# Third mixture of experts: where its zeros, edge rows, edge products and returned rows stand

## The chip, the cores and the metric

One core of a Trainium2 chip. The time is device microseconds of one launch; a kernel is compared by the median over runs. The profile is one execution taken by the hardware profiler; its times are microseconds from the start of the span unless marked ns. Engines: PE (TensorE, matmul), DVE (VectorE), ACT (ScalarE), POOL (GpSimd, which also issues indirect DMAs), SP (SyncE, which issues DMAs).

## The reference

The reference is a four-layer graph network over N = 2708 nodes with D = 256 features; every layer is a graph step over the dense adjacency and a feed-forward step, both added to x. The change lies in layer 2 (the third):

```python
x = x + _L2_gnn_ref(_layernorm(x), adj, W, a)        # one-head graph attention
x = x + _L2_ffn_ref(_layernorm(x)[None], ...)[0]      # mixture of 4 experts, this case

h = x @ W_gat                                          # (M, 4 heads, 4 experts)
e = leaky_relu(a_src[src] + a_dst[dst])                # over listed edges and self loops
alpha = segment softmax of e over dst
agg = segment_sum(h[src] * alpha, dst) + b_gat
scores = layernorm(agg).reshape(M, 4, 4).mean(1)
topk_s, topk_i = top_k(scores, 2);  w = softmax(topk_s)
for ei in range(4):
    g = where(topk_i == ei, w, 0).sum(-1)
    hh = gelu(x @ W1[ei] + b1[ei])                     # 256 -> 512
    out += g[:, None] * (hh @ W2[ei] + b2[ei])         # 512 -> 256
```

Layer 3 then starts with a four-head attention, whose values are prepared inside this mixture.

## The kernel before

The nodes lie in 22 tiles of 128 rows (the last has 20), and work goes by CHUNKS: five chunks of 512 nodes and one of 148. x stays in SBUF the whole time (k.x). The program is written once and then scheduled: a scheduler fixes, before anything runs, the order of the instructions on each engine, from the order in the text, the data dependencies and its own estimates. On the chip each engine goes through its list in that order and stops at an instruction whose inputs aren't there. So where an instruction stands in an engine's list can differ from where it stands in the text.

The parts that the change and the prediction touch, in order of time:

- **Before the one-head pass.** `load_x` (L71) reads x from the table `acc` in DRAM, that the mixture of layer 1 scatters into; each of its seven loads waits for the one two before it. `GatFront.all` norms x (L1641 to L1655), transposes it (`ft_ps`, L1610) and multiplies with the attention's weights (`v_ps`, L3447); the weights' last columns are made by DVE from `w` and the rows `ar` (L3432, L3438). `Deal.__init__` fills a zero tile on POOL (L4035) and has POOL write it to twelve places in DRAM: row 0 of four tables `fd` (L4040) and eight tables `z` of 512 rows (L4042).
- **The one-head pass** (`fast_gat`): for each chunk DVE makes the weights PT from the adjacency tile `aj` (L3551), PE multiplies (`acc_ps`, L3650), DVE normalizes and adds to x (L3686). Eight `aj` tiles and ten PT tiles are in turn.
- **Edge part of the mixture** (`scores_listed`). All edges that need it are in 16 columns of 128 rows (OW = 16). For each, POOL gathers a row of R from DRAM into `Rd` and one of T into `G` (L3855), 32 gathers in all, in two groups of Q = 8 columns. Then, per group, DVE forms `wq` (L3926), `msg` (L3867) and for each column an X of 128x440 (L3931), and PE adds them up in `e_ps` (L3939), 16 products. `S` (L3947), the norms, the two highest scores per node, and `Deal.rank` (L4108 to L4190) follow; they give the gates and the slots. `last_used` makes a flag that decides the branch at L4356, by which the fourth expert is skipped when no node picked it.
- **Experts.** `up` makes `h_ps` (L4266) and applies gelu on ACT (L4273); `down` makes `y_ps` (L4283), one tile of 128x256 per block of 128 nodes, in two buffers. Expert 0 runs on all six chunks while the edge part is going on; its results, and those of experts 1 and 2 on chunk 0, are parked: `park` copies y_ps by ACT (L4300) and adds the bias on POOL (L4301). The gathers wait in three places for a parked row: `scores.send` hands in a parked column, from which DVE makes a zero that is added to the row numbers (L3850, L3851).
- **Units.** For chunks 1 to 4 experts 1 and 2 run only on the rows dealt to them: eight units (c, i) of 384 or 256 rows. A unit gathers its rows (`xe`, L4196), transposes them (L4370), runs `up` and `down`, and for each block of y DVE adds the bias (`ys`, L4415) and POOL scatters it to `z` (L4210). `back(c)` loads both z of a chunk (`zt`, L4383, on SP), and `plus` adds its rows to x by DVE (L4344). In between `side` works off the steps of layer 3's values (L3483, L3447, L3453), a few at a time, one chunk after another, as soon as a chunk's x is complete.

Of the kernel before, what the change touches and what calls it, by code (L numbers as in the profile page):

```python
# [29 lines left out]
def blocks(c0, cs):  # L30

    return [((c0 + o) // 128, o, min(128, cs - o)) for o in range(0, cs, 128)]
# [3700 lines left out]
def scores_listed(k, fT, w, edges, agg, pool):  # L3733
# [3 lines left out]

    nc, tc = k.nc, k.tc
    H, E = 4, 4
    W = E + 2
# [3 lines left out]
    with ExitStack() as pc, tc.tile_pool(name="sp", bufs=1) as pp, tc.tile_pool(  # L3747
# [90 lines left out]
        for c0 in range(0, OW, Q):  # L3838
            for src, idx, out in (
                (Rt, edges.odst, Rd),  # L3840
                (Tt, edges.osrc, G.rearrange("p c h w -> p c (h w)")),
            ):


                at = idx[:, c0 : c0 + Q]
                done = yield
                if done is not None:
                    at = tmp.tile([128, Q], I32, name="at_idx")
                    no = tmp.tile([128, 1], I32, name="no")
                    nc.vector.tensor_tensor(no, done, done, ALU.is_lt)  # L3850
                    nc.vector.tensor_tensor(  # L3851
                        at, idx[:, c0 : c0 + Q], no.to_broadcast([128, Q]), ALU.add
                    )
                for c in range(Q):
                    nc.gpsimd.indirect_dma_start(  # L3855
                        out=out[:, c0 + c, :],
                        out_offset=None,
                        in_=src,
                        in_offset=bass.IndirectOffsetOnAxis(
                            ap=at[:, c : c + 1], axis=0  # L3860
                        ),
                        bounds_check=NT * 128 - 1,
                        oob_is_err=False,
                    )
# [48 lines left out]
        )  # L3913
        acc = ps.tile([128, NT, H * (E + 1)], F32, name="e_ps")
        for c0 in range(0, OW, Q):
            cc = slice(c0, c0 + Q)
            dlo = tmp.tile([128, Q, 128], F32, name="dlo")
            nc.vector.tensor_tensor(
                dlo,
                io[:, None, :].to_broadcast([128, Q, 128]),  # L3920
                edges.olo[:, cc, None].to_broadcast([128, Q, 128]),
                ALU.is_equal,
            )
            wq = tmp.tile([128, Q, H], F32, name="wq")
            msg = tmp.tile([128, Q, H, E + 1], F32, name="msg")
            nc.vector.tensor_tensor(wq, Rd[:, cc, :], G[:, cc, :, E + 1], ALU.max)  # L3926
            times(msg, wq, G[:, cc, :, : E + 1], Q)
            for c in range(Q):
                X = tmp.tile([128, NT, H * (E + 1)], F32, name="X")
                shp = [128, NT, H * (E + 1)]  # L3930
                nc.vector.tensor_tensor(  # L3931
                    X,
                    dhi[:, c0 + c, :, None].to_broadcast(shp),
                    msg[:, c, :, :]
                    .rearrange("p h w -> p (h w)")[:, None, :]
                    .to_broadcast(shp),
                    ALU.mult,
                )
                nc.tensor.matmul(  # L3939
                    acc.rearrange("p t w -> p (t w)"),  # L3940
                    lhsT=dlo[:, c, :],
                    rhs=X.rearrange("p t w -> p (t w)"),
                    start=(c0 + c == 0),
                    stop=(c0 + c == OW - 1),
                )
# [74 lines left out]
class Deal:  # L4020
# [8 lines left out]
    S = 5  # L4029

    def __init__(self, k, dram, pool):
        nc = k.nc
        self.k = k
        zero = pool.tile([128, 4, D], F32, name="zero")
        nc.gpsimd.memset(zero, 0.0)  # L4035
        self.fd, self.z = [], []
        for c in range(len(self.C)):
            self.fd.append(dram.tile([513, D], F32, name=f"fd{c}"))
            self.z.append([dram.tile([512, D], F32, name=f"z{c}{i}") for i in range(2)])
            nc.gpsimd.dma_start(self.fd[c][0:1, :], zero[0:1, 0, :])  # L4040
            for z in self.z[c]:
                nc.gpsimd.dma_start(z.rearrange("(t p) d -> p t d", p=128), zero)  # L4042
# [177 lines left out]
def fast_l2_ffn(k, w, edges, deal, then):  # L4220
# [7 lines left out]
    with ExitStack() as ctx:  # L4228
# [14 lines left out]
        ps1 = ctx.enter_context(tc.tile_pool(name="ps_m1", bufs=3, space=PSUM))  # L4243
        ps2 = ctx.enter_context(tc.tile_pool(name="ps_m2", bufs=2, space=PSUM))
        first = yp.tile([128, NT, D], F32, name="y0")
        whole = {e: yp.tile([128, 4, D], F32, name=f"y{e}") for e in (1, 2)}
        b1 = bp.tile([128, E, M], F32, name="b1")
        b2 = bp.tile([128, E, D], F32, name="b2")
        for e in range(E):
# [29 lines left out]
        def down(e, hT, bl, use):  # L4279
            for t, o, n in bl:  # L4280
                y = ps2.tile([128, D], F32, name="y_ps")
                for m in range(M):
                    nc.tensor.matmul(  # L4283
                        y[:n],
                        lhsT=hT[:, m, o : o + n],
                        rhs=wts[e][1][:, m, :],
                        start=(m == 0),
                        stop=(m == M - 1),
                    )
                use(t, n, y)  # L4290
                next(side[0], None)

        def expert(e, c0, cs, use):
            hT = up(e, lambda kk: fT[:, kk, c0 : c0 + cs], cs)
            down(e, hT, blocks(c0, cs), use)

        def park(e, dst):
            def use(t, n, y):
                yt = dst[:n, t, :]
                nc.scalar.copy(yt, y[:n])  # L4300
                nc.gpsimd.tensor_tensor(yt, yt, b2[:n, e, :], ALU.add)  # L4301

            return use

# [8 lines left out]
        with tc.tile_pool(name="el", bufs=1) as pl, tc.tile_pool(  # L4313
            name="eh2", bufs=2
        ) as hot, tc.tile_pool(name="ps_el", bufs=1, space=PSUM) as ps:
            deal.prepare(keep, pl, hot)
            bank = ps.tile([128, 512], F32, name="deal_ps")
            agg = pl.tile([128, NT, 4, 4], F32, name="agg")
            scores = scores_listed(k, fT, w, edges, agg, pl)
            next(scores)  # L4320
            next(scores)

            pace = iter((3, 4, 7))
            at = next(pace)
            for c0, cs in CHUNKS:
                expert(0, c0, cs, park(0, first))
                while at is not None and at < c0 // 128 + 4:
                    scores.send(first[:, at, :1])
                    at = next(pace, None)
            for _ in scores:  # L4330
                pass
            scores_norm(k, w, agg, sc, pl)
            top2_dense(k, sc, E, gates, pl)
            wts.update({e: load(e) for e in (2, 3)})
            for c in deal.rank(gates, bank):
                for i in range((2, 1, 0, 0)[c]):
                    xes[c, i] = gathered(c, i)
            last_used(k, gates[:, :, E - 1], flag, pl, deal.ids[:, 3, :1])
            for e in (1, 2):
                expert(e, *CHUNKS[0], park(e, whole[e]))  # L4340

        def plus(src, t, n, e):
            xt = k.x[:n, t, :]
# [47 lines left out]
        def drain():  # L4391
            for _ in side[0]:
                pass

        own(*CHUNKS[0])
        for e in (1, 2):
            for t in range(4):
                plus(whole[e][:, t, :], t, 128, e)
        side[0] = steps(*CHUNKS[0])
        units = [(c, i) for c in range(4) for i in range(2)]  # L4400
        xT = turn(*units[0])
        zs = {}
        for u, (c, i) in enumerate(units):
# [15 lines left out]
            xT = xT_next  # L4419
            if i == 1:  # L4420
                zs[c] = back(c)
            elif c > 0:
                drain()
                for j in range(2):
                    for t in range(4):
                        plus(zs[c - 1][j][:, t, :], deal.C[c - 1][0] // 128 + t, 128, 1 + j)
                side[0] = steps(*deal.C[c - 1])
        own(*CHUNKS[-1])
        expert(1, *CHUNKS[-1], add(1))
        drain()  # L4430
        for j in range(2):
            for t in range(4):
                plus(zs[3][j][:, t, :], deal.C[3][0] // 128 + t, 128, 1 + j)
        side[0] = steps(*deal.C[3])
        expert(2, *CHUNKS[-1], add(2))
        drain()
        for _ in steps(*CHUNKS[-1]):
            pass
# [417 lines left out]
def model(tc, I, out):  # L4856
# [4 lines left out]
    with tc.tile_pool(name="flags", bufs=1) as fp:  # L4861
# [4 lines left out]
        with ExitStack() as ctx:  # L4866
            k = Fast(ctx, tc, I["x"], bad, adjT)
            with tc.tile_pool(name="lists", bufs=1) as lp:
# [36 lines left out]
                with ExitStack() as c2:  # L4905
                    keep = c2.enter_context(tc.tile_pool(name="g2", bufs=1))
                    with tc.tile_pool(name="g2t", bufs=1) as tmp:
                        front = GatFront(k, I["L2_gnn_W"], I["L2_gnn_a"], 1, keep, tmp)
                        front.all(tmp)
                        front.ready(2)  # L4910
                    deal = Deal(k, dealt, keep)
                    fast_gat(k, adjT, front, True)
                c3 = ctx.enter_context(ExitStack())
                right = dict(side="right")
                keep = c3.enter_context(tc.tile_pool(name="g3", bufs=1, **right))
# [96 lines left out]
```

## Time and profile before

| | us |
|---|---|
| median of three runs | 2414.18 (2412.02 to 2417.53) |
| the profiled execution | 2414.3 |
| its span | 2412.5 |
| PE busy in it | 2235.9 |
| DVE busy in it | 1529.4 |
| ACT, POOL busy in it | 713.8, 444.2 |
| PE busy from 1485.0 to 1757.4 (the mixture) | 241.4 of 272.4 |
| PE busy from 1617.6 to 1757.4 (from the branch on) | 119.8 of 139.8 |
| PE busy from 1250.0 to 1440.0 (the one-head pass) | 189.95 of 190.0 |

A window's row gives its length, then for each engine the busy time and, in brackets, the number of instructions, then the granted PE clock, the DMA engines' busy share and the rate in GB/s. A wait's row gives the engine and line that waited, the engine and line that it waited for, and total, times and longest in us. In a timeline a row is a group of like instructions: start, length, engine, line, operation, tile written, tiles read, shape, count, and in brackets the idle time before it and what ended that. An engine that stands idle costs something only if PE, in the end, waits for it.

### The profile page before, as it was taken

The page shows a single profiled execution, that of the slowest core. Times are in us where ns is not written, and L with a number is a line of the kernel's source. Part 1 is how long each engine was busy: PE and PEld are TensorE (multiplying, and loading weights), DVE is VectorE, ACT ScalarE, POOL GpSimd, SP SyncE. Part 2 cuts the span into 40 slices and gives each one's busy share as a digit, 9 for nine tenths or more (in the row PEclk, how much of TensorE's full clock was granted, in tenths as well). Part 3 has the DMA queues.
Part 4 walks back from the last instruction along what each step waited for, and adds up shares of the span by engine and source line. Part 5 has one row for each costly group of instructions (what it writes and reads, how often), then busy time and mean ns, then how long its engine had stood idle before and what let it go on. Part 6 is the DMA issues. An engine that isn't in the chain of part 4 may idle for free. (4 is left out here: it accounts for less than half of the span.)

```text
span 2412.5 us, 32100 instructions
## 1 busy us (share of the span) xinstructions
PE 2235.9 (93%) x11600; PEld 1493.6 (62%) x11600; DVE 1529.4 (63%) x3453; ACT 713.8 (30%) x1499; POOL 444.2 (18%) x482
## 2 busy tenths in 40 slices
PE   7999999988899899999689998988899999959996
PEld 4777765677778676777568886647632333326664
DVE  7588878645676557456555554183489998854544
ACT  6433343213655222212150003333451112211221
POOL 1000013004100243565300001623100000012221
PEclk9999999869999999999889996999999999979998
DMA  5244332200756244332345535012233333324430
GB/s 150 66 114 118 110 79 78 74 1 12 236 172 191 62 115 97 82 75 49 106 147 146 144 84 102 13 40 75 66 90 104 109 112 110 92 69 146 134 116 15
DMA packets 168111, 235.23 MB, mean 98 GB/s; under 512 B 32125, under 2 KB 101475, under 8 KB 167940
## 3 DMA queue, kind: packets, MB, share of 16 engines
q1 hardware_dynamic: 130320, 184.03, 26.3%
q0 software_dynamic: 18688, 32.97, 6.1%
q10 hardware_dynamic: 18932, 16.05, 2.1%
q8 instruction: 95, 1.56, 0.3%
q14 instruction: 76, 0.62, 0.1%
HBM read 200.31 MB, written 33.74 MB: 97 GB/s over the span
## 5 line engine op out<-in xcount | busy, mean ns | idle before, releaser
L3551 DVE SCALAR_TENSOR_TENSOR PT<-Rr,Q,aj 128x512 f32<-128x512 f32 (+3 forms) x630 | 395.2, 680 | 102.6 <-PE acc_ps L3650 78.5
L3725 PE MATMUL acc_ps<-PT,V 128*64 128x512 f32 (+4 forms) x2016 | 333.3, 551 | 0.1
L3725 PEld LDWEIGHTS acc_ps<-PT,V 128*64 128x64 f32 (+1 forms) x2016 | 94.0, 122 | 210.2 <-issue 158.3
L1845 PE MATMUL acc_ps<-fa,PT 128*128 128x257 f32 x882 | 215.4, 383 | 1.2 <-DVE out L1865 1.2
L1845 PEld LDWEIGHTS acc_ps<-fa,PT 128*128 128x128 f32 x882 | 163.9, 190 | 66.5 <-issue 33.8
L3650 PE MATMUL acc_ps<-V,PT 128*128 128x257 f32 x882 | 194.3, 381 | 0.8 <-issue 0.8
L3650 PEld LDWEIGHTS acc_ps<-V,PT 128*128 128x128 f32 x882 | 166.2, 190 | 27.9 <-issue 1.7
L3305 PE MATMUL h_ps<-xT,w1t 128*128 128x384 f32 x512 | 176.9, 498 | 2.8 <-ACT xT L3296 2.8
L3322 PE MATMUL y_ps<-w2t,hT 128*128 128x256 f32 x768 | 169.8, 380 | 0.0
L2512 PE MATMUL acc_ps<-V,at 128*128 128x257 bf16 x1323 | 158.4, 279 | 9.3 <-DVE at L2503 7.3
L3322 PEld LDWEIGHTS y_ps<-w2t,hT 128*128 128x128 f32 x768 | 144.9, 190 | 21.1
L2512 PEld LDWEIGHTS <-at 128*128 128x128 bf16 x1323 | 129.9, 100 | 32.7 <-issue 4.9
L3305 PEld LDWEIGHTS h_ps<-xT,w1t 128*128 128x128 f32 x512 | 96.0, 193 | 67.8 <-ACT xT L3296 7.6
L1817 ACT ACTIVATE PT<-s_ps,rq 128x512 f32<-128x512 f32 (+1 forms) x126 | 79.5, 637 | 174.3 <-PE s_ps L1793 168.7
L3334 POOL DMA_INDIRECT acc<-ys,ids x48 | 91.8, 1912 | 157.6 <-DVE ys L3331 121.2
L1793 PE MATMUL s_ps<-KT,QT 128*128 128x512 f32 (+1 forms) x252 | 116.2, 548 | 2.5 <-ACT PT L1817 1.6
L1818 DVE SCALAR_TENSOR_TENSOR PT<-aj,PT 128x512 f32<-128x512 int32 (+1 forms) x126 | 79.1, 633 | 57.8 <-ACT PT L1817 57.5
L3004 POOL DMA_INDIRECT xe<-fd,idg x48 | 79.7, 1660 | 195.4 <-DVE early_f L3035 181.1
L4806 PE MATMUL y_ps<-w2t,hT 128*128 128x256 f32 (+1 forms) x512 | 112.8, 379 | 0.0
L3312 ACT ACTIVATE hT<-h_ps,b1t 128x384 f32<-128x384 f32 x128 | 74.3, 581 | 115.1 <-PE h_ps L3305 113.7
L4755 POOL DMA_INDIRECT xe<-fd,idg x32 | 32.4, 1013 | 410.2 <-DVE ids L4726 400.9
L4283 PE MATMUL y_ps<-w2t,hT 128*128 128x256 f32 (+1 forms) x432 | 101.8, 385 | 5.7 <-DVE ys L4415 5.6
(800 smaller groups left out, 3509.8 us busy)
## 6 DMA issues: line engine op xcount, KB each, us to landing
aj<-in_adjT SPq DMA_DIRECT2D x399, 256.0 KB
w1t<-in_L_ffn_W SPq DMA_DIRECT2D x8, 1024.0 KB
w2t<-in_L_ffn_W SPq DMA_DIRECT2D x8, 1024.0 KB
w1t<-in_L_ffn_w SPq DMA_DIRECT2D x8, 1024.0 KB
w2t<-in_L_ffn_w SPq DMA_DIRECT2D x8, 1024.0 KB
fd<-fa ACTq DMA_DIRECT2D x13, 512.0 KB
aj<-in_adjT SPq DMA_DIRECT2D x63, 74.0 KB
aj<-in_adjT SPq DMA_DIRECT2D x21, 202.0 KB
```

Source lines behind the costliest of these rows:

```text
L1793: nc.tensor.matmul(s[:, :cs], lhsT=QT[:, j * 128 : j * 128 + 128], rhs=KT[:, c0 : c0 + cs], start=True, stop=True,)
L1845: nc.tensor.matmul(ac, lhsT=PT[:, o : o + n], rhs=fa[:, j, :], start=j == 0, stop=False)
L2512: nc.tensor.matmul(ac[:, c:], lhsT=at[:, o : o + n], rhs=V[:, j, r], start=j == 0 and q == 0, stop=False, skip_group_check=True,)
L3004: nc.gpsimd.indirect_dma_start(out=xe[:, i, :], out_offset=None, in_=self.fd[:rows, :], in_offset=bass.IndirectOffsetOnAxis(ap=idx[:, i : ...
L3305: nc.tensor.matmul(hp, lhsT=w1t[:, kk, m * 128 : (m + 1) * 128], rhs=self.xT[:, kk, :], start=(kk == 0), stop=(kk == 1),)
L3322: nc.tensor.matmul(y, lhsT=self.hT[:, m, i * 128 : (i + 1) * 128], rhs=w2t[:, m, :], start=(m == 0), stop=(m == M - 1),)
L3334: add = nc.gpsimd.indirect_dma_start(out=acc, out_offset=bass.IndirectOffsetOnAxis(ap=self.ids[:, i : i + 1], axis=0), in_=ys, in_offset=None,
L3551: nc.vector.scalar_tensor_tensor(PT, R, Q, aj, ALU.max, ALU.mult)
L3650: nc.tensor.matmul(ac[:n], lhsT=PT[:, o : o + n], rhs=V[:, j, 0, :], start=(j == 0), stop=False,)
L3725: nc.tensor.matmul(w.pop("out"), **w)
L4283: nc.tensor.matmul(y[:n], lhsT=hT[:, m, o : o + n], rhs=wts[e][1][:, m, :], start=(m == 0), stop=(m == M - 1),)
L4806: nc.tensor.matmul(y[:n], lhsT=hT[:, m, o : o + n], rhs=w2t[:, m, :], start=(m == 0), stop=(m == M - 1),)
```

## The change

Four things are written differently:

1. The zero tile and the twelve writes move from `Deal.__init__` to a method `clear`, called after the one-head pass in the text. The tile is made by DVE from x of tiles 12 to 15 (a comparison that is never true), so that it can't be made before chunk 3 of that pass is done.
2. The gathers of edge rows no longer wait for parked rows.
3. The edge products, in their two groups, are written behind expert 0's third and fourth chunk (i = 2 and 3), and a hold (`issue_after`) puts what they issue on PE behind the last matmul of that chunk. Parking is one DVE addition from y_ps instead of an ACT copy and a POOL addition.
4. A chunk's returned rows are added at the end of its next chunk's second unit instead of its first. Expert 2 on chunk 0 is no longer parked; it is computed after the units, with chunk 0's own rows, and the value steps of chunk 0 come last but one instead of first.

```diff
@@ scores_listed
                 at = idx[:, c0 : c0 + Q]
-                done = yield
-                if done is not None:
-                    at = tmp.tile([128, Q], I32, name="at_idx")
-                    no = tmp.tile([128, 1], I32, name="no")
-                    nc.vector.tensor_tensor(no, done, done, ALU.is_lt)
-                    nc.vector.tensor_tensor(
-                        at, idx[:, c0 : c0 + Q], no.to_broadcast([128, Q]), ALU.add
-                    )
                 for c in range(Q):
                     nc.gpsimd.indirect_dma_start(
...
         for c0 in range(0, OW, Q):
+            if c0:
+                yield
             cc = slice(c0, c0 + Q)
@@ Deal
     def __init__(self, k, dram, pool):
-        zero = pool.tile([128, 4, D], F32, name="zero")
-        nc.gpsimd.memset(zero, 0.0)
+        self.zero = pool.tile([128, 4, D], F32, name="zero")
...
+    def clear(self, done):
+        nc, zero = self.k.nc, self.zero
+        nc.vector.tensor_tensor(zero, done, done, ALU.is_lt)
+        for c in range(len(self.C)):
             nc.gpsimd.dma_start(self.fd[c][0:1, :], zero[0:1, 0, :])
             for z in self.z[c]:
                 nc.gpsimd.dma_start(z.rearrange("(t p) d -> p t d", p=128), zero)
@@ fast_l2_ffn
-        whole = {e: yp.tile([128, 4, D], F32, name=f"y{e}") for e in (1, 2)}
+        second = yp.tile([128, 4, D], F32, name="y1")
...
         def park(e, dst):
             def use(t, n, y):
-                yt = dst[:n, t, :]
-                nc.scalar.copy(yt, y[:n])
-                nc.gpsimd.tensor_tensor(yt, yt, b2[:n, e, :], ALU.add)
+                nc.vector.tensor_tensor(dst[:n, t, :], y[:n], b2[:n, e, :], ALU.add)
...
             next(scores)
-            next(scores)
-            pace = iter((3, 4, 7))
-            at = next(pace)
-            for c0, cs in CHUNKS:
-                expert(0, c0, cs, park(0, first))
-                while at is not None and at < c0 // 128 + 4:
-                    scores.send(first[:, at, :1])
-                    at = next(pace, None)
-            for _ in scores:
-                pass
+            for i, (c0, cs) in enumerate(CHUNKS):
+                last = expert(0, c0, cs, park(0, first))
+                if i in (2, 3):
+                    with tc.issue_after(last.ins):
+                        next(scores, None)
...
-            for e in (1, 2):
-                expert(e, *CHUNKS[0], park(e, whole[e]))
+            expert(1, *CHUNKS[0], park(1, second))
...
-        own(*CHUNKS[0])
-        for e in (1, 2):
-            for t in range(4):
-                plus(whole[e][:, t, :], t, 128, e)
-        side[0] = steps(*CHUNKS[0])
+        def put_back(c):
+            drain()
+            for j in range(2):
+                for t in range(4):
+                    plus(zs[c][j][:, t, :], deal.C[c][0] // 128 + t, 128, 1 + j)
...
             if i == 1:
                 zs[c] = back(c)
-            elif c > 0:
-                drain()
-                for j in range(2):
-                    for t in range(4):
-                        plus(zs[c - 1][j][:, t, :], deal.C[c - 1][0] // 128 + t, 128, 1 + j)
-                side[0] = steps(*deal.C[c - 1])
+                if c:
+                    put_back(c - 1)
+                    side[0] = steps(*deal.C[c - 1])
+        own(*CHUNKS[0])
+        for t in range(4):
+            plus(second[:, t, :], t, 128, 1)
+        expert(2, *CHUNKS[0], add(2))
+        put_back(3)
+        side[0] = chain(steps(*deal.C[3]), steps(*CHUNKS[0]))
         own(*CHUNKS[-1])
-        expert(1, *CHUNKS[-1], add(1))
-        drain()
-        for j in range(2):
-            for t in range(4):
-                plus(zs[3][j][:, t, :], deal.C[3][0] // 128 + t, 128, 1 + j)
-        side[0] = steps(*deal.C[3])
-        expert(2, *CHUNKS[-1], add(2))
+        for e in (1, 2):
+            expert(e, *CHUNKS[-1], add(e))
         drain()
@@ model
                     deal = Deal(k, dealt, keep)
                     fast_gat(k, adjT, front, True)
+                    deal.clear(k.x[:, 12:16, :])
```

More of the change, by code (lines that the diff above doesn't have):

```diff
@@ L4031, in __init__ @@
     def __init__(self, k, dram, pool):
-        nc = k.nc
         self.k = k
-        zero = pool.tile([128, 4, D], F32, name="zero")
-        nc.gpsimd.memset(zero, 0.0)
+        self.zero = pool.tile([128, 4, D], F32, name="zero")
         self.fd, self.z = [], []
@@ L4282, in down @@
                 for m in range(M):
-                    nc.tensor.matmul(
+                    last = nc.tensor.matmul(
                         y[:n],
@@ L4291, in down @@
                 next(side[0], None)
+            return last
         def expert(e, c0, cs, use):
             hT = up(e, lambda kk: fT[:, kk, c0 : c0 + cs], cs)
-            down(e, hT, blocks(c0, cs), use)
+            return down(e, hT, blocks(c0, cs), use)
         def park(e, dst):
             def use(t, n, y):
-                yt = dst[:n, t, :]
-                nc.scalar.copy(yt, y[:n])
-                nc.gpsimd.tensor_tensor(yt, yt, b2[:n, e, :], ALU.add)
+                nc.vector.tensor_tensor(dst[:n, t, :], y[:n], b2[:n, e, :], ALU.add)
             return use
```

## The prediction

> **What bounds the kernel now.** The page first: the span is 2412.5 us of the profiled execution's 2414.3 us, and PE is busy for 93% of it. So the end is set by PE's work and by the places where PE stands. The page's chain of waits holds 1% of the span and doesn't help. I therefore went stage by stage: the windows, then the waits of a stage, then the timeline of one engine. The change touches three stretches: the front of the one-head pass (1184 to 1249 us), that pass (to 1457 us), and the third mixture (1485 to 1757 us).
>
> The front, by windows (busy us of each engine, granted clock, DMA share, GB/s), then two of its waits (total, times, longest):
>
> ```profile
> 1192.00:1196.00 4.00, 0.00 (x0) 0.00 (x0) 0.00 (x0) 0.00 (x0) 3.14 (x6) 0.50 1.00 254
> 1200.00:1204.00 4.00, 0.00 (x0) 0.00 (x0) 2.85 (x14) 1.58 (x2) 0.00 (x0) 0.50 1.04 403
> 1204.00:1208.00 4.00, 1.94 (x8) 1.55 (x8) 1.47 (x9) 2.90 (x6) 0.00 (x0) 0.50 1.04 387
> ```
> ```profile
> DVE ln_st L1641 <- DMA x<-acc: 17.6, 3, 12.9
> PEld v_ps L3447 <- DVE w L3438: 4.1, 1, 4.1
> ```
>
> PE does nothing until 1205.5, the DMA engines are full, and DVE waits for x. POOL issues the eight 512 KB zero writes from 1188.7 to 1197.5, in the same microseconds as the 2.8 MB of x.
>
> The mixture: POOL's edge rows, DVE's two waits for them, PE's first chunks and two later stalls (start, us, engine, line; in brackets the idle time before and who ended it):
>
> ```profile
> 1499.91 1.12 POOL L3855 DMA_INDIRECT Rd<-Rt,odst  x1 [249.14 <-DMA Rt<-R]
> 1501.33 1.02 POOL L3855 DMA_INDIRECT Rd<-Rt,odst  x1 [0.30 <-issue]
> ...
> 1522.76 1.00 POOL L3855 DMA_INDIRECT G<-Tt,at_idx  x1 [0.31 <-issue]
> ...
> 1550.25 1.00 POOL L3855 DMA_INDIRECT G<-Tt,at_idx  x1 [0.30 <-issue]
> ```
> ```profile
> 1525.39 0.21 DVE L3926 TENSOR_TENSOR wq<-Rd,G 128x32 f32<-128x32 f32 x1 [12.04 <-issue]
> ...
> 1552.72 0.74 DVE L3926 TENSOR_TENSOR wq<-Rd,G 128x32 f32<-128x32 f32 x1 [10.63 <-DMA G<-Tt,at_idx]
> ```
> ```profile
> 1489.21 10.04 PE L4266 MATMUL h_ps<-fT,w1t 128*128 128x512 f32 x16
> 1499.08 7.07 PE L4283 MATMUL y_ps<-w2t,hT 128*128 128x256 f32 x32
> 1505.99 7.03 PE L4266 MATMUL h_ps<-fT,w1t 128*128 128x512 f32 x16
> 1512.86 7.07 PE L4283 MATMUL y_ps<-w2t,hT 128*128 128x256 f32 x32
> ...
> 1617.65 0.66 PE L4370 MATMUL xt_ps<-ident,xe 128*128 128x128 f32 x2 [5.93 <-PEq L4356]
> ...
> 1660.62 3.78 PE L4283 MATMUL y_ps<-w2t,hT 128*128 128x256 f32 x8 [5.55 <-DVE ys L4415]
> ```
>
> Read three things. Edge rows leave POOL every 1.30 us, and a row is in use 2.5 us after its issue (1522.76 to 1525.39, 1550.25 to 1552.72). DVE stands 12.0 and 10.6 us for them, yet PE runs through both, because here ACT empties y_ps (L4300) and POOL adds the bias (L4301). And where DVE does own the eviction (L4415), a DVE wait for zt stops PE for 5.55 us.
>
> [...] here 16 instructions took 10.04 us at 1489 after sparse work and 7.03 us at 1506, 3.0 us dearer. [...]
>
> **Part 1, zeros moved.** Before: a 0.95 us POOL fill and 12 POOL writes (0.8 to 1.1 us each) at the front. After: one DVE operation over 128x1024 when chunk 3's x are ready, and the 12 writes behind it. What leaves the front is 4.2 MB; at the 387 to 403 GB/s seen that is 10.6 us of DMA time. Step by step: the first x load is issued at 1190.5 and landed at 1199.4. The fifth, with little beside it, went from 1209.45 to 1213.44, 4.0 us. At that pace the first is in at about 1194.5, the third and fourth (each waits for the load two before it) at about 1198, the fifth at 1201.5. The weights' ar rows, issued between them, come some 10 us earlier as well, and they hold the first v_ps (the 4.1 us wait). From v_ps at 1215.9 to the pass PE is nearly always busy, so the gain there carries through: **-10.5 us**. Not below -13 (the zeros' own time and a little), not above -6 (the first load alone). The zeros' new place: chunk 3's last x is written at 1407, and chunk 4's and 5's adjacency then asks for little (70, then 38 GB/s, DMA share 0.27 and 0.16 from 1410 to 1430). DVE's 1.2 us (dlo, as large, took 1.22) falls into a stretch with 0.98 us idle per tile and ten PT buffers; POOL has nothing else there from 1251 to 1499, and its queue reaches the edge rows long after. **+0.5 us**, bounds 0 and +4, by two late adjacency tiles.
>
> **Part 2, edge rows and evictions.** Removed: three waits for parked rows and their DVE index sums (0.16 + 0.17 us each, off the path); 30 ACT copies of 0.37 us and 30 POOL adds of 0.73 us. Added: 26 DVE evictions of 0.42 us (the row of L4415) for them. The order in which the built programs hold DVE's instructions is what counts. After: four evictions of chunk 0; wq for the first 16 rows, msg, three X; **one** eviction of chunk 1; wq for the second 16 rows, msg; then the next seven evictions. The new line "yield" and the hold behind the last matmul bind PE's products alone; the sums in front of them have been drawn up. With two y_ps buffers PE can be two blocks ahead of DVE. Rows first: unpaced they leave from 1499.91 every 1.30 us; the 16th issues at 1519.5 and is usable at 1522.0, the 32nd at 1540.3 and 1542.9. PE in chunk 1, at the rate of before: blocks 0 and 1 done by 1516.6. Block 2 needs the eviction of block 0, behind the first wq: 1522.0 + 2.3 (wq to the third X, as 1525.39 to 1527.66) + 0.4 = 1524.8: PE stands 8.2 us. Block 3 needs the eviction of block 1, behind the second wq: 1542.9 + 0.6 + 0.4 = 1544.0; block 2 ends at 1526.6: PE stands 17.4 us. Restart at half clock: 3.2 us. **+28.8 us**; bounds +24 (no clock loss and rows 2 us earlier) and +32. The 16 products themselves keep their 12.1 us, only in two halves. Nothing covers this stall: what could run, chunks 2 to 5, is behind block 3 in PE's order.
>
> **Part 3, gating chain.** It now runs beside chunks 4, 5 and one expert (13.8 + 5.9 + 13.8 = 33.5 us) where it had two (27.6). L3432/L3438, 3.3 us of DVE, have moved in front of the pass; four evictions and table switches have moved in. PE lost 1.23 + 0.79 us to it, and about 3 us more to its small matmuls; I take **-1.0**, bounds -3 and +2. The branch's 5.93 us stay. Behind it DVE has one row addition instead of three and no POOL add (1.67 us) before the xT copy (2.35 us on PE): **-1.8**, bounds -2.3 and 0.
>
> **Part 4, units.** Expert 2 on chunk 0 (13.8 us of PE) and chunk 0's value steps (5.4 us) move to the end: the same work, 0 by itself. The adds of zt are written one unit later, but in the built order they still stand ahead of evictions: one of zt's rows before the second eviction of unit (0,1), zt1's before the first of unit (1,0), all four of the third pair before both of unit (2,1). Each zt is ready 5.2 to 5.8 us after the last scatter's issue ends (1641.9 to 1647.7, 1654.2 to 1659.4), and scatters of one table come 3.2 us apart. With the steps gone from the first two units PE arrives sooner and waits longer. Walking the three pairs through, against 5.55, 1.78 and 2.79 us of PE stall before, I get -2.0, -0.7 and +1.6: **-1.2** (the last 0.1 is rounding), bounds -9 (nearly all three stalls go) and +6. The tail, two steps beside 11.7 us of work instead of one: 0, bounds -3 and +4.
>
> **Sum.** -10.5 + 0.5 + 28.8 - 1.0 - 1.8 - 1.2 = +14.8 us on the profiled 2414.3, so 2429.1; the median of three runs is 2414.18, 0.1 below, and I forecast **2429.0 us**. A measurement here can tell about 0.2%, 4.8 us.
>
> **Rivals.** (a) *DVE's wait doesn't hold PE, faster:* if the 32nd row is usable by about 1517, before block 2 of chunk 1, part 2 is nearly 0 and the sum is -14: 2400 us. The turning point is a stall of 14 us. For it: the pacing may itself have stretched the rows. Against: eight in a row were unpaced at 1499.91 and still 1.30 us apart. 0.07. (b) *The units get what they are written for:* 10.1 us of stalls go and half the clock loss doesn't come: 2419 us, no change that can be told. 0.11. (c) *The front keeps its time,* because loads of x wait on each other: +25 us, 2439 us. For it: the loads are chained in pairs. Against: 254 to 403 GB/s were moving while they waited. 0.14. (d) *The edit does not do what it says:* the adds still stand where they did; that is in my own case. My case 0.68.
>
> **Range.** 2415 to 2440: the low end is -13 at the front, +24 for the stall and -8 in the units, the rest as above; the high end is just past rival (c). Faster 0.08, same 0.11, slower 0.81.
>
> **What would show it.** Right: PE idle of some 8 and 17 us inside chunk 1 with DVE's wq as what came before, both released by G's rows; a span from PE's first h_ps to the branch about 14 us longer although an expert has left it; x in and v_ps started 10 us earlier, counted from the last scatter of the mixture before. Wrong: PE busy through chunk 1; adjacency waits behind the zeros; zt no longer among DVE's waits.

## The result, and the profile after

The changed kernel takes **2429.4 us** (median of 10 runs, 2422.4 to 2434.6), the kernel before 2413.5 us in the same series: a ratio of 1.0065, 95% interval 1.0052 to 1.0079. It is slower by 15.9 us. The profiled execution of after has a span of 2426.2 us and a mean PE clock of 0.951, as before.

First the front. Windows of after (length, busy us and instructions of PE, PE's weight loads, DVE, ACT, POOL, then granted clock, DMA share, GB/s):

```profile
1190.00:1194.00 4.00, 0.00 (x0) 0.00 (x0) 3.77 (x18) 1.78 (x3) 0.00 (x0) 0.50 0.99 287
1194.00:1198.00 4.00, 3.05 (x15) 2.98 (x16) 3.44 (x13) 2.77 (x6) 0.00 (x0) 0.50 0.84 269
1198.00:1202.00 4.00, 1.20 (x5) 0.70 (x4) 3.67 (x16) 0.97 (x3) 0.00 (x0) 0.50 0.30 78
```

And two waits of after (us in total, times, longest):

```profile
DVE ln_st L1641 <- DMA x<-acc: 8.2, 1, 8.2
...
PEld v_ps L3447 <- DVE w L3438: 3.2, 1, 3.2
```

The first x load is issued at 1185.97 here, so a window starting at 1194 corresponds to one at 1198.5 before. PE already works in it, and by 1202 the DMA engines have come down to 0.30. DVE waits for x once, 8.2 us, where it waited three times and 17.6 us. From the first x load to the first product of the pass it was 59.18 us (1190.50 to 1249.68) and is 47.86 us (1185.97 to 1233.83): 11.3 us gained. The 4.5 us by which everything here begins earlier were there before the change acts; over the eleven profiled executions of this study that first load is issued between 1181.4 and 1190.5.

Now the mixture. POOL's edge rows, then DVE, then PE in expert 0's first chunks (start, us, engine, line, operation, tiles, and in brackets the idle time before and who ended it):

```profile
1484.84 1.12 POOL L3844 DMA_INDIRECT Rd<-Rt,odst  x1 [80.50 <-DMA Rt<-R]
1486.26 1.03 POOL L3844 DMA_INDIRECT Rd<-Rt,odst  x1 [0.30 <-issue]
...
1504.49 1.00 POOL L3844 DMA_INDIRECT G<-Tt,osrc  x1 [0.30 <-issue]
...
1525.73 1.00 POOL L3844 DMA_INDIRECT G<-Tt,osrc  x1 [0.30 <-issue]
```
```profile
1507.20 0.22 DVE L3917 TENSOR_TENSOR wq<-Rd,G 128x32 f32<-128x32 f32 x1 [16.55 <-DMA G<-Tt,osrc]
1507.45 0.32 DVE L3856 TENSOR_TENSOR msg<-G,wq 128x160 f32<-128x160 f32 x1
1507.81 1.67 DVE L3922 TENSOR_TENSOR X<-dhi,msg 128x440 f32<-128x440 f32 x3
1509.40 0.42 DVE L4295 TENSOR_TENSOR y<-y_ps,b 128x256 f32<-128x256 f32 x1
1528.18 0.21 DVE L3917 TENSOR_TENSOR wq<-Rd,G 128x32 f32<-128x32 f32 x1 [18.37 <-DMA G<-Tt,osrc]
1528.43 0.33 DVE L3856 TENSOR_TENSOR msg<-G,wq 128x160 f32<-128x160 f32 x1
1528.67 0.75 DVE L4295 TENSOR_TENSOR y<-y_ps,b 128x256 f32<-128x256 f32 x2
```
```profile
1496.88 3.62 PE L4278 MATMUL y_ps<-w2t,hT 128*128 128x256 f32 x16
1509.87 3.78 PE L4278 MATMUL y_ps<-w2t,hT 128*128 128x256 f32 x8 [9.37 <-DVE y L4295]
1529.15 3.44 PE L4278 MATMUL y_ps<-w2t,hT 128*128 128x256 f32 x8 [15.50 <-DVE y L4295]
1532.42 7.03 PE L4261 MATMUL h_ps<-fT,w1t 128*128 128x512 f32 x16
```

Read the three together. The 16th row leaves POOL at 1504.49 and DVE goes on at 1507.20; the 32nd leaves at 1525.73, DVE goes on at 1528.18. Both blocks of the 16 instructions at 1496.88 are done by 1500.50, and DVE stands idle from 1490.64 to 1507.20; still it doesn't empty the first before 1509.40, behind the wq that stands ahead in its list. Between the two waits it empties that single y_ps, and at 1509.87 PE does one single block. PE stands 9.37 and 15.50 us, and the two blocks after the stops take 3.78 and 3.44 us where half of the 16 instructions at 1496.88 took 1.81: some 3.6 us of slow clock on top. Where each stretch stands, cut in both traces at the same instructions:

| us | before | after | difference |
|---|---|---|---|
| first x load to the pass | 59.18 | 47.86 | -11.3 |
| the pass and the features, to expert 0's first h_ps | 239.53 | 240.56 | +1.0 |
| first h_ps to layer 3's first attention product (L3725) | 268.18 | 294.78 | +26.6 |

With the 4.5 us of an earlier start the product at L3725 begins 11.8 us later (1757.39 to 1769.17), and the span is 13.7 us longer.

### The profile page after: what moved, and what is told of

The parts are those of the page before. It is cut to its first block, busy times and chain, and to the rows that moved or that the text cites. A ratio compares the mean times of both kernels' runs of the same rounds, so it can differ in the third digit from the quotient of the medians.

```text
span 2426.2 us, 32066 instructions
## 1 busy us (share of the span) xinstructions
PE 2236.2 (92%) x11600; PEld 1491.3 (61%) x11600; DVE 1537.9 (63%) x3478; ACT 703.0 (29%) x1471; POOL 425.2 (18%) x451
## 5 line engine op out<-in xcount | busy, mean ns | idle before, releaser
L3725 PE MATMUL acc_ps<-PT,V 128*64 128x512 f32 (+4 forms) x2016 | 334.0, 551 | 0.0
L3725 PEld LDWEIGHTS acc_ps<-PT,V 128*64 128x64 f32 (+1 forms) x2016 | 94.3, 123 | 210.4 <-issue 159.0
L4278 PE MATMUL y_ps<-w2t,hT 128*128 128x256 f32 (+1 forms) x432 | 108.3, 402 | 37.1 <-DVE y L4295 27.8
L4278 PEld LDWEIGHTS y_ps<-w2t,hT 128*128 128x128 f32 (+1 forms) x432 | 82.1, 196 | 56.4 <-DVE y L4295 29.5
L1818 DVE SCALAR_TENSOR_TENSOR PT<-aj,PT 128x512 f32<-128x512 int32 (+1 forms) x126 | 79.3, 634 | 57.8 <-ACT PT L1817 57.5
L3004 POOL DMA_INDIRECT xe<-fd,idg x48 | 79.7, 1660 | 196.0 <-DVE early_f L3035 181.6
L4792 PE MATMUL y_ps<-w2t,hT 128*128 128x256 f32 (+1 forms) x512 | 112.8, 379 | 0.0
```

Source lines behind the costliest of these rows:

```text
L3004: nc.gpsimd.indirect_dma_start(out=xe[:, i, :], out_offset=None, in_=self.fd[:rows, :], in_offset=bass.IndirectOffsetOnAxis(ap=idx[:, i : ...
L3725: nc.tensor.matmul(w.pop("out"), **w)
L4278: last = nc.tensor.matmul(y[:n], lhsT=hT[:, m, o : o + n], rhs=wts[e][1][:, m, :], start=(m == 0), stop=(m == M - 1),)
L4792: nc.tensor.matmul(y[:n], lhsT=hT[:, m, o : o + n], rhs=w2t[:, m, :], start=(m == 0), stop=(m == M - 1),)
```

## The experiments

Every ratio is to the kernel before, run beside it on the same chip, and isn't exactly the quotient of two medians; a ratio's hundredth of a per cent is 0.24 us. e1, e2, e3 and e5 ran on one chip and the others on another, so versions are best compared by their ratios and their traces.

**e1_park_act: DVE keeps its waits, but not the evictions.**

```diff
@@ park, of the kernel after
-                nc.vector.tensor_tensor(dst[:n, t, :], y[:n], b2[:n, e, :], ALU.add)
+                yt = dst[:n, t, :]
+                nc.scalar.copy(yt, y[:n])
+                nc.gpsimd.tensor_tensor(yt, yt, b2[:n, e, :], ALU.add)
```

> Part 2 undone on the eviction side alone: the kernel after, but each parked block leaves y_ps by an ACT copy and gets its bias by a POOL addition, as before. DVE's two waits for edge rows stay as they are, 16.6 and 18.4 us in the profile of after. Theory (a DVE wait holds PE only because DVE owns the eviction): the stalls of 9.4 and 15.5 us in chunk 1 go, with some 3 us of lost clock, so about 2402 us (2398 to 2406), and the trace shows DVE still standing 15 to 20 us twice while PE works. Rival 1 (unpaced gathers slow PE or its operands, whoever empties y_ps): 2425 to 2430. Rival 2 (PE would stand at the edge products instead, because they wait for the same rows): some 10 us come back there, about 2412.

Measured: 2400.8 us, ratio 0.9959 (0.9944 to 0.9973). DVE and PE in its trace:

```profile
1503.20 0.22 DVE L3917 TENSOR_TENSOR wq<-Rd,G 128x32 f32<-128x32 f32 x1 [23.17 <-DMA G<-Tt,osrc]
...
1523.67 0.73 DVE L3917 TENSOR_TENSOR wq<-Rd,G 128x32 f32<-128x32 f32 x1 [18.18 <-DMA G<-Tt,osrc]
```
```profile
1494.81 7.07 PE L4278 MATMUL y_ps<-w2t,hT 128*128 128x256 f32 x32
1501.72 7.03 PE L4261 MATMUL h_ps<-fT,w1t 128*128 128x512 f32 x16
1508.58 7.07 PE L4278 MATMUL y_ps<-w2t,hT 128*128 128x256 f32 x32
1515.49 2.38 PE L3930 MATMUL e_ps<-X,dlo 128*128 128x440 f32 x6
1526.30 6.49 PE L3930 MATMUL e_ps<-X,dlo 128*128 128x440 f32 x10 [8.43 <-DVE X L3922]
```

DVE still stands 23.2 and 18.2 us (16.6 and 18.4 in after), and PE works through chunks 1 and 2 in 7.07 and 7.03 us a piece. So the rows themselves don't slow PE; the eviction behind the wait does. Rival 2 is there as well: the fourth X of the first group stands behind the second wq in DVE's list, and PE stops 8.43 us at the products (each X gives two of the instructions counted here). First h_ps to L3725 takes 272.51 us, 22.3 less than after, with that stop in it. The total is as the first theory had it.

**e2_hold_dve: DVE keeps the evictions, and the sums stand behind them.**

```diff
@@ fast_l2_ffn, of the kernel after (park now also appends its instruction to parked)
-                    with tc.issue_after(last.ins):
+                    with tc.issue_after(last.ins), tc.issue_after(parked[-1].ins):
                         next(scores, None)
```

> Part 2 kept, with DVE still doing the evictions, but the sums are held on DVE too: each group of wq, msg and X stands behind the last parked block of chunk 2 and of chunk 3, not only its PE products behind that chunk's last matmul. Theory (the place of wq in DVE's list is the whole fault, not DVE evictions, not unpaced rows): no stall in chunk 1, about 2402 us (2398 to 2407); wq of the second group waits for rows under 1 us, since the 32nd row is usable near 1528 and chunk 3 ends near 1533. Rival (DVE, with evictions and sums together, becomes the bound in chunks 3 and 4, eight X of 0.7 us and more standing ahead of four evictions): stalls of 5 to 8 us there, 2408 to 2411 us. If neither: 2425 and more, and DVE's place isn't the cause.

Measured: 2398.2 us, ratio 0.9938 (0.9916 to 0.9959). DVE in chunk 3, and PE:

```profile
1520.93 0.42 DVE L4296 TENSOR_TENSOR y<-y_ps,b 128x256 f32<-128x256 f32 x1 [1.30 <-PE y_ps L4278]
...
1522.84 0.21 DVE L3917 TENSOR_TENSOR wq<-Rd,G 128x32 f32<-128x32 f32 x1
...
1523.45 5.29 DVE L3922 TENSOR_TENSOR X<-dhi,msg 128x440 f32<-128x440 f32 x8
1535.49 0.42 DVE L4296 TENSOR_TENSOR y<-y_ps,b 128x256 f32<-128x256 f32 x1 [6.76 <-PE y_ps L4278]
```
```profile
1520.73 3.60 PE L4261 MATMUL h_ps<-fT,w1t 128*128 128x512 f32 x8
1524.17 6.12 PE L3930 MATMUL e_ps<-X,dlo 128*128 128x440 f32 x16
1530.13 3.60 PE L4261 MATMUL h_ps<-fT,w1t 128*128 128x512 f32 x8
1533.56 7.07 PE L4278 MATMUL y_ps<-w2t,hT 128*128 128x256 f32 x32
```

The first wq now has no wait at all (nor has the second, at 1542.14), and the eight X fit beside half an `up`: DVE waits for PE, not PE for DVE. First h_ps to L3725 takes 266.08 us, 28.7 less than after. The loss of part 2 is the place of two groups of sums, each with a waiting wq at its head, in one list. Beyond part 1 the change isn't shown to pay even so: e2, with all four parts, stands at 0.9938, part 1 alone (e3, next) at 0.9962, a difference of 5.8 ± 6.4 us.

**e3_zeros: part 1 alone, on the kernel before.** The diff is that of `Deal` and of the call of `clear` in the section on the change.

> The kernel before with part 1 alone: zeros made and written in the one-head pass. Theory (front -10.5, pass +0.5 as forecast; the two traces gave -11.3 and +1.0): 2403.3 us (2401 to 2406), a ratio of 0.9957. Rival (c) of the forecast, the front keeps its time because the loads of x wait on each other: 2413 to 2414, no change.

Measured: 2400.9 us, ratio 0.9962 (0.9946 to 0.9977), 9.2 us less at 2413.5, where the theory had 0.9957. First x load to the pass: 49.88 us (1184.70 to 1234.58), 9.3 less than before. Rival (c) falls.

**e5_units: part 4 alone, on the kernel before.** The diff is that of the loop of units and of what stands behind it.

> The kernel before with part 4 alone: returned rows written one unit on, expert 2 on chunk 0 and chunk 0's value steps at the end. Theory 1 (the forecast's sum for the units): -1.2, so 2412.3 us. Theory 2 (the traces of before and after, 136.05 us and 152.9 - 13.8 us from the branch to layer 3): +3.0, 2416.5 us. Rival (the units get what they are written for): -8 to -10, 2404 to 2406 us. Most of it lies within what five rounds can tell only for the rival and for theory 2; the stalls of PE ahead of y_ps in the units, 10.1 us before, decide between them.

Measured: 2417.2 us, ratio 1.0025 (1.0016 to 1.0035). The number is that of theory 2, but not its place. PE ahead of the units:

```profile
1587.99 0.41 PE L4108 MATMUL deal_ps<-d_sel,d_every 128*128 128x32 f32 x2 [1.58 <-DVE d_sel L4105]
...
1593.39 0.37 PE L4176 MATMUL deal_ps<-d_hv,d_hl 128*128 128x10 bf16 x8 [4.77 <-DVE d_hl L4169]
...
1597.16 0.36 PE L4176 MATMUL deal_ps<-d_hv,d_hl 128*128 128x10 bf16 x8 [2.20 <-DVE d_two L4185]
...
1607.89 0.88 PE L4369 MATMUL xt_ps<-ident,xe 128*128 128x128 f32 x3 [4.36 <-DVE x L4343]
```

With the edge part where it was before, expert 2 on chunk 0 was the cover of the gating chain. Once it has left, PE stops for each step of that chain: stops over 0.6 us add up to 17.4 us there, against 10.3 before. In the kernel after the chain has chunks 4 and 5 beside it, so this loss isn't in it.

**e7_hold_units_old: e2 with part 4 undone.**

> The kernel with the sums held on DVE (e2), but part 4 undone: expert 2 on chunk 0 back in front of the branch, rows added one unit sooner, chunk 0's steps first. It separates part 4's units from what its moved expert covers. Theory: in e5 the chain of gates lost its cover (PE stands 17.4 us there against 10.3), which can't happen here, where chunks 4 and 5 run beside it; so only the units' stalls count, 15.1 us of PE in e2's trace against 12.7 in before: e7 is 2 to 3 us faster than e2, 2395 to 2396 us. Rival: part 4 costs the 4.8 us of e5 in the units themselves, so 2393 to 2394. Other rival: part 4 pays once the sums are held, 2400 and more.

Measured: 2398.2 us, ratio 0.9935 (0.9921 to 0.9948), beside e2's 0.9938: no difference that can be told. From the units' first h_ps to L3725, the moved expert's 13.8 us counted out, e2 takes 140.0 us and e7 137.6; e7 gives it back ahead of that, where the xT copy stops PE for 4.45 us (0.65 in e2) and the branch for 1.97 (3.65). With the sums held, part 4 as built neither pays nor costs by more than some 6 us; the 2 to 3 us that were expected lie within that.

**e9_hold_back: e2, and the returned rows held behind the evictions.**

```diff
@@ loop of units, of e2 (ys' instruction is appended to parked)
                 if c:
-                    put_back(c - 1)
+                    with tc.issue_after(parked[-1].ins):
+                        put_back(c - 1)
```

> e2 plus the delay that part 4 was written for, now on the chip: inside the loop of units the additions of returned rows stand behind the last eviction of the unit that they are written after. Theory (the waits for zt ahead of evictions make the units' stalls): the stalls of 3.9, 1.95 and 1.8 us of PE ahead of y_ps go, DVE waits for zt fall from about 36 us to under 10, so 6 to 8 us under e2: 2390 to 2393 us. Rival (eight additions in one burst, 8 x 0.45 us, stand ahead of the next evictions and the xT copy instead): half of the gain, 2394 to 2396 us. Rival (DVE's waits there are off the path): 2398, no change from e2.

Measured: 2381.2 us, ratio 0.9877 (0.9862 to 0.9892). The additions of e2's first pair, then of e9's:

```profile
1614.61 0.48 DVE L4334 SCALAR_TENSOR_TENSOR x<-zt,gates,x 128x256 f32<-128x256 f32 x1 [7.43 <-DMA zt<-z]
1622.66 0.88 DVE L4334 SCALAR_TENSOR_TENSOR x<-zt,gates,x 128x256 f32<-128x256 f32 x2 [5.72 <-DMA zt<-z]
```
```profile
1623.44 0.42 DVE L4406 TENSOR_TENSOR ys<-y_ps,b 128x256 f32<-128x256 f32 x1 [1.30 <-PE y_ps L4278]
1623.78 3.25 DVE L4334 SCALAR_TENSOR_TENSOR x<-zt,gates,x 128x256 f32<-128x256 f32 x8
```

And the stretch from the branch to L3725 in both (columns as above), e2 first:

```profile
1586.96:1742.42 155.46, 135.39 (x581) 101.34 (x581) 67.32 (x217) 61.24 (x120) 42.31 (x52) 0.95 0.20 60
```
```profile
1583.50:1722.90 139.40, 130.47 (x582) 97.91 (x582) 67.77 (x217) 61.83 (x120) 43.05 (x52) 0.98 0.22 67
```

The stretch is 16.1 us shorter: 11.1 us of PE's idle time (20.07 to 8.93) and 4.9 us of PE's busy time, for 581 and 582 instructions, while the mean granted clock rises from 0.95 to 0.98. DVE's waits for zt fall from 43.4 to 7.0 us. The expectation had the mechanism and missed the size: it counted three stops and left out the slow clock that came with them, and it left out two more stops that went too, 2.31 us ahead of the transposes and 3.44 us in expert 2 on chunk 0. By the ratios the gain on e2 is 14.7 ± 6 us.

**e10_hold_both: the last pair held as well.**

```diff
@@ behind the units, of e9 (add's ys is appended to parked too)
-        put_back(3)
+        with tc.issue_after(parked[-1].ins):
+            put_back(3)
```

> e9 with the last pair of returned rows held too, behind the last eviction of expert 2 on chunk 0. Theory: the stall of 3.4 us of PE in expert 2 on chunk 0 goes, and chunk 4's value steps, which start after it, still have the two experts on the last chunk and the steps of chunk 0 beside them: 2 to 3 us under e9, 2388 to 2391 us. Rival (the value steps start too late and lengthen the tail before layer 3 by as much): the same as e9. If the tail has no cover at all: 2 to 4 us slower than e9.

Measured: 2379.5 us, ratio 0.9864 (0.9849 to 0.9879). That is the lowest median of this study, 1.4% under before; against e9 the intervals overlap, so the 2 to 3 us expected are neither shown nor refuted (the 2388 to 2391 us started from a slower e9). The stop that it was meant to remove had already gone in e9. What its trace shows less of is PE's waiting in the value steps, 1.1 us in stops over 0.6 us from the units to L3725's preparation against 4.2 in e9 (2.49 and 1.72): first h_ps to L3725 takes 246.92 us, in e9 249.75. There is no sign of a tail left without cover.

**e11_hold_old: part 1 and that hold alone, without the unit of delay.**

> The kernel before with part 1 (zeros in the pass) and one thing more: at the old place, one unit sooner than part 4 has it, the additions of returned rows stand behind the last eviction of the first unit of the next chunk. No other part of the change. It asks whether the gain of e9 needs the unit of delay at all, or only the place in DVE's list. Theory (the place alone): the three stalls of PE seen with part 1 alone, 5.55, 1.80 and 2.76 us, go with the clock that they cost (in e9, 11.1 us of idle time took 4.9 us of clock with them), 10 to 15 us under the 2401 us of part 1 alone: 2386 to 2391 us. Rival (without the delay the rows are not back: a zt is ready some 5.5 us after the last scatter, so DVE waits behind the evictions and the next unit's xT copy waits with it): 2394 to 2398 us, DVE waits for zt of 10 us and more.

Measured: 2390.4 us, ratio 0.9900 (0.9883 to 0.9918). The only zt wait that its trace has left on DVE:

```profile
DVE x L4349 <- DMA zt<-z: 3.1, 1, 3.1
```

The three stops are gone: the place in the list is what removes them, and the rows are back in time one unit sooner too. The stretch from the branch to L3725 (columns as above), e3 first:

```profile
1602.32:1746.57 144.25, 122.41 (x534) 93.79 (x535) 63.64 (x207) 57.33 (x115) 41.28 (x57) 0.91 0.21 65
1598.52:1735.96 137.44, 122.89 (x534) 92.58 (x535) 64.08 (x208) 59.09 (x117) 41.53 (x57) 0.90 0.22 68
```

It is 6.8 us shorter, and all of that is idle time of PE (21.84 to 14.55). The slow clock that was to go with the stops stays, at a mean of 0.90 against 0.91, and PE has new stops of 3.01 and 2.26 us in the value steps. The total came out in the expected range, but this trace explains only part of it. The delay of part 4 without the hold gave nothing that can be told (e7). The hold without the delay pays: e11 against e3, 15 ± 6 us by the ratios, 10.5 by the medians. Whether the delay adds to the hold stays open: by the ratios the hold gives 14 ± 5 us with it (e9 against e7), and from first h_ps to L3725 the traces have 16.0 us with it and 7.0 without.

**e6_three_y: three y_ps buffers and two h_ps buffers in the kernel after.**

> The kernel after with three y_ps buffers and two h_ps buffers instead of two and three. Theory from the rule of the forecast alone (PE can be as many blocks ahead of DVE as there are y_ps buffers, list of DVE unchanged): the stalls of chunk 1 shrink from 24.9 to about 18 us, 2422 us. Theory from the built order: the third buffer lets the scheduler draw wq up by one eviction more (three evictions, wq, one, msg and X, wq, eight), so the same two blocks of chunk 1 stand, until about 1508 and 1529 counted as in after: stalls of about 7.5 and 19.5 us, the time as after, 2428 to 2431 us. Rival (two h_ps buffers make ACT's gelu a new bound): above 2433.

Measured: 2420.3 us, ratio 1.0038 (1.0027 to 1.0048), below both theories, nearest to the first one's number. PE in chunk 1:

```profile
1507.92 3.78 PE L4278 MATMUL y_ps<-w2t,hT 128*128 128x256 f32 x8 [5.25 <-DVE y L4295]
1528.95 3.56 PE L4278 MATMUL y_ps<-w2t,hT 128*128 128x256 f32 x8 [17.25 <-DVE y L4295]
1532.34 7.03 PE L4261 MATMUL h_ps<-fT,w1t 128*128 128x512 f32 x16
```

The stops end where the built order said, near 1508 and 1529, and chunk 2 starts at 1532.34, as in after (1532.42). So the third buffer brought 1 us at most in chunk 1 (chunk 2 starts 57.0 us after the first h_ps, 58.0 in after); the stops add up to 22.5 us, since PE came there 2.2 us later. Most of the 6.5 ± 4 us by which this is faster than after lie elsewhere: stops between expert 1 and the units add up to 2.1 us here and 5.4 in after, and the rest wasn't traced to a place. With two buffer counts changed at once, this run doesn't say more.

## Why the prediction was right, point by point

The forecast was 2429.0 us, range 2415 to 2440, slower with 0.81. Its steps:

| step | forecast | shown |
|---|---|---|
| front | -10.5 | -11.3 (traces), -9.2 (e3, -13.0 to -5.6) |
| zeros in the pass | +0.5 | not to be told |
| stall in chunk 1 | +28.8 (8.2 + 17.4 + 3.2) | +28.5 (9.4 + 15.5 + 3.6); e2 against after -28.7 |
| chain and xT copy | -1.0 - 1.8 | -4.7 |
| units | -1.2 | +3.0 by the traces; e2 against e7 +0.7 ± 6 |

**Front.** Right in mechanism, and in size as far as it can be told. v_ps starts 15.43 us after the first x load (1201.40), before 25.43: 10.0 us sooner, as was to be seen; the other 1.3 us lie between v_ps and the pass. From the first x load to the pass it is 57.5 and 59.2 us in the two profiles with the zeros in front (e5, before) and 47.9 to 50.1 in the other nine, a gain of 7.5 to 11.3 us. The stretch of the pass varies between 238.8 and 242.7 us over the eleven profiles, e5 without zeros in it being at 241.8, so the +1.0 of the zeros can't be told from nothing. The writes themselves do what was said: from 1396 on, POOL otherwise idle, and PE busy for 189.95 of 190.0 us of the pass as before.

```profile
1396.13 0.52 POOL L4035 DMA_DIRECT2D fd<-zero  x1 [160.09 <-DVE zero L4033]
1396.64 1.57 POOL L4037 DMA_DIRECT2D z<-zero  x2
```

**Stall.** The step that decided. Which block stands, behind which wq and for which row came out as walked through; the rows left every 1.30 us and were usable 2.7 and 2.5 us after issue. Counted from expert 0's first h_ps, the two blocks were to start at +35.6 and +54.8 us, and they start at +35.5 and +54.8. (The walk's two sums are each written 0.1 us too high: 1522.0 + 2.3 + 0.4 is 1524.7, and 1542.9 + 0.6 + 0.4 is 1543.9. It changes nothing here.) The single terms are off by 1 to 2 us in opposite directions: the first stop is longer because PE came there sooner (chunk 0's h_ps took 8.91 us instead of 10.04), the second shorter because the block ahead of it ran at half clock (3.78 us) and ended later. The slow clock was 3.6 us, 1.97 and 1.63, where 3.2 were set. That 3.2 was the author's estimate; the 10.04 us at 1489 and 7.03 us at 1506 in before differ by 3.0. That "sparse work" slows the clock isn't shown: from 1460 to 1470 of before it was 0.50 as well, with PE busy for 9.96 of 10.00 us. In after the granted clock, the third number from the end, is 0.50 from 4.3 us after PE began to stand until 3.0 us into the second block:

```profile
1504.81:1532.12 27.31, 6.75 (x15) 4.97 (x16) 3.76 (x10) 0.00 (x0) 17.04 (x17) 0.50 0.06 4
```

Rival (a) is refuted by e1 and e2 together: with DVE's wait but without the eviction behind it the stall goes, and with the eviction but without the wait it goes as well. Rival (b) fell as well: the stops in the units of after are 2.17, 4.13 and 4.20 us, no less in sum than before's 5.55, 1.78 and 2.79; they go only in e9.

**Chain and branch.** Mis-sized. "The branch's 5.93 us stay" was wrong. PE's stops there, after:

```profile
1609.54 2.76 PE L4278 MATMUL y_ps<-w2t,hT 128*128 128x256 f32 x8 [2.97 <-DVE y L4295]
1614.49 0.45 PE L4357 MATMUL xt_ps<-ident,xe 128*128 128x128 f32 x1 [1.77 <-PEq L4343]
1615.59 0.90 PE L4357 MATMUL xt_ps<-ident,xe 128*128 128x128 f32 x3 [0.65 <-DVE xT L99]
```

That is 5.4 us; with 0.26 us at the small products 5.6, against 10.3 before, so -4.7 where -2.8 was forecast. The xT copy came as forecast (2.35 us of PE before, 0.65 after, so -1.7 where -1.8 was set); the branch is the term that was off. From the first h_ps to the branch it is 140.1 us, 11.7 longer than before, where 14 was forecast. The branch cost PE 1.77 us, but DVE stood 4.54 us ahead of two evictions, ended by something that the trace gives as remote, and passed 2.97 of it to PE. What that is, stays open.

**Units.** Here the sum failed. Pair by pair it had -2.0, -0.7 and +1.6; the stops moved by +0.75 (2.17 + 4.13 against 5.55), -1.8 and +1.4. The first pair was mis-sized: the forecast put one zt addition ahead of an eviction, and DVE's wait for it, 7.28 us, also held back the xT copy, a second stop of 2.17 us. The remaining 2.6 us of the +3.0 are in no stop over 0.6 us. They are busy time of PE: from the units' first h_ps to L3725 it is 135.75 of 152.89 us in after and 118.47 of 136.05 before, so 3.5 us more with the moved expert's 13.8 taken off, against 0.4 us less idle time. The mean granted clock there is 0.94 in after and 0.95 before; that it is the cause isn't shown. The reading that the additions "still stand where they did" was right: DVE waits 36.1 us for zt in after and 29.7 in before, and e9 shows what it was worth.

The parts were sized with one profiled execution each, and a stretch in which nothing is changed moves by some 2 to 4 us between executions; that the forecast's sum is within 1 us of the median is partly luck. The chain came out 1.9 us better than forecast and the units 4.2 us worse, and these two errors cancel in part.

## What to carry to other kernels

Where an engine empties the accumulators that PE needs next, ask of every wait ahead of those evictions in that engine's list how long it can last: here DVE's wait for two groups of gathered rows cost 28.7 us, and with the same instructions some places further back the loss was gone (e2). A statement that stands later in the text is not later in the list; when a scheduler fixes the order, a hold belongs on the engine whose wait is to be kept back, not only on the one that consumes the result. And the clock can count with the stops: taking away 11.1 us of PE's idle time took 4.9 us of busy time with it in e9, and taking away 7.3 us took none in e11.

## What the runs showed that was not expected

- A skipped branch has no fixed price on PE: 5.93 us in before, 1.77 in after, 0.99 to 4.00 in the other versions whose traces name it, the branch in the program being the same. In after a stop of DVE stood ahead of it.
- A stop of 1.95 us in e2 was followed by a block of 3.51 us for 8 instructions, one of 1.82 us in the same trace by a block of 1.99 us. The granted clock stayed at 1.00 behind a stop of 2.79 us in before (1711.10 to 1716.00) and behind one of 2.17 us in after (1645.55 to 1651.58); behind one of 4.13 us in after, which ended at 1652.71, it was 0.50 (1651.58 to 1658.41). At some 2 us the length of the stop alone doesn't tell whether slow work follows. The half clock lasted 6.83 us there and 27.31 us, four times as long, in chunk 1 of after.
